# The last image's opening and end, a projection written by halves, and the outputs in other parts: one edit of a two-layer convolution kernel

## Chip, cores and metric

The kernel runs on one core of a Trainium2 chip. The metric is the device time of one launch in microseconds (us). A core has TensorE (PE, matmuls; PEld is its weight loads), VectorE (DVE), ScalarE (ACT), GpSimd (POOL) and SyncE (SP, which here only issues DMAs), each with its own instruction stream. They meet through semaphores and share the on-chip memory SBUF; matmul results arrive in PSUM, eight banks of 512 fp32 values on each of 128 partitions.

## What is computed

The input x has 4 images of 256 channels and 48 x 48 pixels. Two layers follow, each added to its input:

```python
# layer 0
h = relu(batch_norm(conv3x3(group_norm(x), conv_w) + conv_b))     # fixed statistics
q, k, v = qkv_w @ h + qkv_b                                       # 8 heads of 32 channels, N = 2304 pixels
a = softmax(q.T @ k * 32**-0.5) @ v
x = x + proj_w @ a + proj_b
# layer 1
g = group_norm(x)
w = conv3x3(g, W_cat)                                             # 45 logits a pixel
outs = [g] + [sum over 9 taps of shift(g, tap * d) * softmax(w[9 of d])[tap] for d in (1, 6, 12, 24, 36)]
y = W_scale @ concat(outs)                                        # 1x1 convolution over 6 * 256 channels
x = x + (y - mean(y)) * rsqrt(var(y) + eps) * gamma + beta        # mean and var over all 4 images
```

The statistics of y run over all images, so no output can be made before the last image's y is finished. Everything is fp32.

## The kernel before, in words

**Halves and chunks.** The 256 channels lie as two halves (index `o` or `h`, `NH` = 2) on 128 partitions. The pixels go in `NCK` = 6 chunks of 8 rows (`CH` = 384 pixels). A tile such as `pp` or `py` is `[P, 2, 512]` or `[P, 3, 512]` in PSUM: half 0 in its first bank, half 1 in its second.

**Order of work.** For each image in turn: attention (`attention`), then the dynamic filters of layer 1 (`dynamic_filters`). During the dynamic filters of images 0 to 2, TensorE also works off the convolution and qkv of the next image (the generator `other`, called through `run` and `fill`). The last image (`alone`) has no such work beside it. The order of all instructions is written out by hand (`manual_schedule`); inside the dynamic filters a small planner (`clock`) keeps a due time for each engine and chooses from them who does what. The semaphore waits are put in by the framework from the tiles that instructions read and write. A fallback for very large scores (`general`) is compiled into the same program, but not run here.

**Attention.** Queries go in 9 units of up to 512; the last unit holds the remaining 256 of both channel halves. In each of 18 key steps, `scores` makes the scores (L954), ScalarE exponentiates them (L962, L963), and `weigh` multiplies by the values (L983). The sum of the exponentials is kept by VectorE in `acc` (L999); in up to five of the steps, part of it is added by a DMA into a scratch tile instead, which L1006 adds later. `sums` (L1015) then sums `acc` over keys with a matmul by ones. In the last unit the last step's exponentials go to `sums` directly. `close` transposes, inverts and multiplies (L1024 to L1034).

**Projection.** `project` (L1067, L1076) makes layer 0's output for one chunk: for both halves two matmuls each, and then for each half the addition of bias and input, its group-norm statistics, and a store. Per image, five of the six chunks are done inside attention, at step 6 of units 3, 5, 7 (two chunks) and 8; the sixth needs the last unit and comes at the opening of `dynamic_filters`.

**Opening of the dynamic filters.** The sixth projection; loading ScalarE's Sqrt table; the group norm's finish (`Norm.finish`: aggregates, two small matmuls into a `misc` bank at L617 to L628, and the inverse root, L87 to L89); loading the Exp table; normalizing (L592); and the first chunk's logits and softmax (`weights`, L1137 onwards). In images 0 to 2, conv work stands in between.

**Taps.** For each chunk, each dilation and each tap: the weight is broadcast into PSUM (`wb`, L1406 or ScalarE's L1403), VectorE multiplies (L1463), GpSimd adds into `cat` (L1480). Three other ways: the first tap writes `cat` (L1437); a *single* product goes to the 1x1 convolution directly; a *split* tap has its second half multiplied and added by VectorE (L1445 to L1449) and its first half added by GpSimd (L1452). A tap is split if GpSimd's due time is past VectorE's by more than `SPLIT` = 4500 ns. `mix` (L1290) is the 1x1 convolution, accumulated in `py`. After the chunk's last one, `done` copies `py` away (L1315, L1317) and takes the statistics (L1323).

**End.** After the last chunk, `finish` aggregates the statistics (L157), makes scale and shift (L87 to L161), and then for images 0 to 3 scales on ScalarE (L1568), adds the residual on VectorE (L1579, L1586) and stores. Images 0 and 1 go in pieces of a channel half (2304 pixels), the first half in pieces of 384. Images 2 and 3 go by chunks. Shortly before, the residual of image 3 and four chunks of image 2's y are loaded (L1500, L1504).

Of the kernel before, what the change touches and what calls it, by code (L numbers as in the profile page):

```python
# [16 lines left out]
N = HH * WW  # L17
P = 128
# [30 lines left out]
def conv_preact_kernel(  # L49
# [98 lines left out]
        nc.vector.tensor_tensor(bn_t, bn_t, vec[:, BN_B, :], ALU.add)  # L148
        return bn_s, bn_t

    def batch_norm_of(yst, pool, tag):

        ymv = pool.tile([P, NH, 2], F32, tag="ymv", name=f"ymv_{tag}")
        ysc = pool.tile([P, NH], F32, tag="ysc", name=f"ysc_{tag}")
        ysh = pool.tile([P, NH], F32, tag="ysh", name=f"ysh_{tag}")
        for o in range(NH):
            nc.vector.bn_aggr(ymv[:, o, :], yst[:, o].rearrange("p c s -> p (c s)"))  # L157
# [374 lines left out]
    with tc.tile_pool(name="w", bufs=1) as wpool, tc.tile_pool(  # L532
# [36 lines left out]
        lg = wpool.tile([P, CH], F32, tag="lg", name="lg")  # L569
        nc.gpsimd.memset(lg, 0.0)  # L570
        yst = wpool.tile([P, NH, B * NCK, 6], F32, tag="yst", name="yst")
        bn_s6 = wpool.tile([P, NH], F32, tag="bn_s6", name="bn_s6")


# [349 lines left out]
        qkv = {}  # L924
        CONV_QKV = MM * (6 * 4 * 6 * TN / CH + NCK * NH * 4 + NT * 2 * C / CH)

        def attention(b, q, k_, vT, pools, spare, project, scratch):


# [39 lines left out]
            def weigh(u, m, p):  # L969
                if m == 0:  # L970
                    state[u] = dict(
                        num=ps_a.tile([P, 512], F32, tag="num", name=f"num_{b}_{u}"),
                        acc=work0.tile([P, 4, QC], F32, tag="acc", name=f"acc_{b}_{u}"),
                    )
                st = state[u]
                several = len(units[u]) > 1
                if several and m == 0:

                    for j, r in enumerate(heads):
                        nc.tensor.matmul(st["num"][r, :], zeros, p[:, j, :], start=True, stop=False)  # L980
                for i, (g, q0, n, at) in enumerate(units[u]):
                    for j, r in enumerate(heads):
                        nc.tensor.matmul(  # L983
                            st["num"][r, at : at + n],
                            vT[:, m, g * P + j * D : g * P + (j + 1) * D],
                            p[:, j, at : at + n],
                            start=(m == 0 and not several),
                            stop=(m == NT - 1 and i == len(units[u]) - 1),
                        )
                end = u == last  # L990
                if end and m == NT - 1:
                    sums(u, p, True, False)
                elif m == 0:
                    st["first"] = p
                else:
                    other = st["first"] if m == 1 else st["acc"]
                    lend = u > 0 and m in LENT[: len(LENT) - end]
                    js = slice(0, 1 if lend else 4)
                    nc.vector.tensor_tensor(st["acc"][:, js], other[:, js], p[:, js], ALU.add)  # L999
# [19 lines left out]
            def close(u):  # L1019

                sums(u, state[u]["acc"], u < last, True)
                st = state.pop(u)
                t = scratch
                nc.vector.transpose(t, st["den"])  # L1024
                rc = work0.tile([P, QC // D], F32, tag="rc", name=f"rc_{b}_{u}")
                nc.vector.reciprocal(rc, t.rearrange("p (k d) -> p k d", d=D)[:, :, 0])
                nc.vector.transpose(
                    t.rearrange("p (k d) -> p k d", d=D),
                    rc.unsqueeze(2).to_broadcast([P, QC // D, D]),
                )  # L1030
                for g, q0, n, at in units[u]:
                    dst = ao[:, g, q0 : q0 + n]
                    src = dst if u < last else st["num"][:, at : at + n]
                    nc.vector.tensor_tensor(dst, src, t[:, at : at + n], ALU.mult)  # L1034
# [27 lines left out]
        def project(b, c, ao, pp, norm):  # L1062

            t = pads[b % 2]
            for o in range(NH):
                for g in range(NH):
                    nc.tensor.matmul(  # L1067
                        pp[:, o, :CH],
                        wp[:, g, o * P : (o + 1) * P],
                        ao[:, g, c * CH : (c + 1) * CH],  # L1070
                        start=(g == 0),
                        stop=(g == NH - 1),
                    )
            for o in range(NH):
                x1 = inside(t, o, c * R, R)
                nc.vector.scalar_tensor_tensor(  # L1076
                    out=x1, in0=rows_of(pp[:, o, :CH]), scalar=pbias[:, o : o + 1], in1=x1,
                    op0=ALU.add, op1=ALU.add,
                )
# [25 lines left out]
        def dynamic_filters(b, ao, chunk, norm, other, pools, beside):  # L1105
# [114 lines left out]
            alone = b == B - 1  # L1220
            ready = {}


            next(beside, None)
            while chunk < NCK:
                project(b, chunk, ao, ps_y.tile([P, 2, 512], F32, tag="y", name=f"pp_{b}_{chunk}"), norm)
                chunk += 1
            table(AF.Sqrt)
            run(2400)
            for at, _ in enumerate(norm.finish(misc)):  # L1230
                if at:
# [2 lines left out]
            for _ in beside:  # L1234
                pass
            table(AF.Exp)

            for r0, r1 in ((0, 2 * R + 1), (2 * R + 1, HH)):
                for h in range(NH):
# [41 lines left out]
            def mix(c, n, o, rhs, last=False, at=None):  # L1281
                def go():
# [13 lines left out]
                        )  # L1296
                    part = 1.0 if at is None else (l1 - l0) * (x1 - x0) / CH
                    clock("PE", NH * MM * part, slot("y", 1) if n == 0 and o == 0 else 0.0)
                    if last and o == NH - 1:
                        done(c)  # L1300
                return go

            def done(c):
                cols = slice(c * CH, (c + 1) * CH)
                if alone:
                    yc = homes[c]
                elif c < NCK - 1:
                    yc = work1.tile([P, NH, CH], F32, tag="y", name=f"y_{b}_{c}", bufs=1)
                of = py.pop(c)[:, :, :CH]
                if c == NCK - 1 and not alone:  # L1310


                    rows = gn[:, :, 1 : 1 + R, 1 : 1 + WW]
                    for o in range(NH):
                        nc.scalar.copy(rows[:, o], rows_of(of[:, o]))  # L1315
                else:
                    nc.scalar.copy(yc, of)  # L1317
                free["y"].append(clock("ACT", 800, clock.t["PE"]))
                if c < NCK - 1:
                    of = yc  # L1320
                    clock("DVE", 1100, free["y"][-1])
                for o in range(NH):
                    nc.vector.bn_stats(yst[:, o, b * NCK + c, :], of[:, o, :])  # L1323
                if alone:
                    return
                if c < NCK - 1:
# [37 lines left out]
            for c in range(NCK):  # L1364
# [21 lines left out]
                for j, (n, at, (k, oy, ox, y0, y1, x0, x1)) in enumerate(taps):  # L1386
# [18 lines left out]
                    else:  # L1405
# [79 lines left out]
                    if j + 1 == len(taps) or taps[j + 1][0] != n:  # L1485
                        for o in range(NH):
# [4 lines left out]
                                    n == len(DILATIONS) - 1,  # L1491
                                ),
                            ))
            while queue:
                fill(when(queue[0]))
                if queue:
# [62 lines left out]

        def finish(work1):  # L1560

            ysc, ysh = batch_norm_of(yst, small, "f")

            def image(b, o):
                return out[b, o * P : (o + 1) * P].rearrange("c r w -> c (r w)")
# [6 lines left out]
            for b, ty, tx in ((0, y_0, x1_0), (1, y_1, x1_1)):  # L1572
                for o in range(NH):

                    n = CH if b == 0 and o == 0 else N
                    for c in range(0, N, n):
                        y = ty[:, o, c : c + n]
                        scaled(y, o)
                        nc.vector.tensor_tensor(y, y, tx[:, o, c : c + n], ALU.add)  # L1579
                        nc.sync.dma_start(out=image(b, o)[:, c : c + n], in_=y)  # L1580
            for b, ty, tx in ((2, y_2, x1_2), (3, homes, x1_3)):
                for c in range(NCK):
                    cols = slice(c * CH, (c + 1) * CH)
# [251 lines left out]
```

## Time and profile before

| | before |
|---|---|
| time, median of 3 runs | 2888.27 us (2886.0 to 2889.01) |
| profiled execution | span 2883.7 us, mean granted TensorE clock 0.981 |
| busy | PE 94%, DVE 83%, ACT 58%, POOL 41% |
| attention of the last image | about 2208 to 2586 us |
| last image's dynamic filters | about 2586 to 2847 us |
| outputs | about 2849 to 2880 us |

A group of instructions in the profile is named by its line, engine, operation and tiles (out<-in), with the number of instructions (x), busy time and mean duration. A timeline row gives start, duration of the merged group, and in brackets how long the engine had been idle and what ended that. fp32 matmuls appear as two records each. PEclk is the clock granted to TensorE, 1.00 being full speed. Idle time counts only where the engine is the one that others wait for.

### The profile page before, as it was taken

The numbers are of one execution on the slowest core, as the hardware profiler recorded it, in microseconds if no ns is written. First come the engines' busy times: TensorE is split into PE (matmuls) and PEld (weight loads), VectorE is DVE, ScalarE is ACT, GpSimd is POOL, SyncE is SP. The second block draws the span as 40 slices with busy tenths as digits, with TensorE's granted clock in tenths as the row PEclk, the third lists the DMA queues.
The fourth block names the chain that finished last, engine by engine and source line by source line (L and its number), as shares of the span: only waits on it lengthen the run. The fifth ranks groups of instructions, "written<-read, shape, count | busy, mean of one in ns | idle before, by whom it ended". The sixth has DMA issues, their size and how long they took to land. (4 is left out here: it accounts for less than half of the span.)

```text
span 2883.7 us, 43644 instructions
## 1 busy us (share of the span) xinstructions
PE 2721.6 (94%) x16950; PEld 1199.6 (42%) x16950; DVE 2381.2 (83%) x2570; ACT 1671.8 (58%) x2105; POOL 1187.6 (41%) x1000
## 2 busy tenths in 40 slices
PE   7999999899999999999999999999999999989994
PEld 5722224556542222455662222355654222244562
DVE  6488888789879988878977898978986988987886
ACT  3488888322349888712238888842234888861124
POOL 1000000798840010399890001079985001006893
PEclk9999999999999999999999999999999999999997
DMA  4524445132353444323225444423223345435225
GB/s 171 126 64 100 98 99 112 48 88 85 71 105 82 103 105 110 78 65 89 54 56 116 98 95 110 100 62 88 65 56 69 75 98 113 100 80 217 57 70 207
DMA packets 148199, 272.94 MB, mean 95 GB/s; under 512 B 66760, under 2 KB 117008, under 8 KB 146192
## 3 DMA queue, kind: packets, MB, share of 16 engines
q0 software_dynamic: 23264, 128.10, 19.5%
q1 hardware_dynamic: 82384, 87.31, 10.8%
q10 hardware_dynamic: 42336, 54.66, 7.5%
q8 instruction: 135, 2.21, 0.3%
q14 instruction: 80, 0.66, 0.1%
HBM read 115.02 MB, written 32.33 MB: 51 GB/s over the span
## 5 line engine op out<-in xcount | busy, mean ns | idle before, releaser
L999 DVE TENSOR_TENSOR acc<-acc,p 128x2048 f32<-128x2048 f32 (+1 forms) x572 | 1061.2, 1855 | 116.3 <-ACT p L963 66.5
L1480 POOL TENSOR_TENSOR cat<-cat,prod 128x752 f32<-128x752 f32 (+9 forms) x661 | 883.3, 1346 | 142.0 <-DVE prod L1463 105.5
L963 ACT ACTIVATE p<-se 128x1536 f32<-128x1536 f32 x648 | 938.5, 1448 | 0.0
L954 PE MATMUL so<-q,k 32*128 32x512 f32 (+1 forms) x1440 | 731.2, 595 | 23.5 <-ACT p L962 17.1
L954 PE MATMUL se<-q,k 32*128 32x512 f32 (+1 forms) x4320 | 740.0, 595 | 0.0
L983 PE MATMUL num<-p,vT 128*32 128x512 f32 (+1 forms) x5760 | 705.4, 562 | 4.3 <-ACT p L963 2.4
L1463 DVE TENSOR_TENSOR prod<-wb,pad 128x384 f32<-128x384 f32 (+8 forms) x687 | 482.7, 737 | 92.7 <-POOL cat L1480 51.3
L962 ACT ACTIVATE p<-so 128x512 f32<-128x512 f32 x648 | 388.4, 599 | 198.1 <-PE se L954 84.7
L954 PEld LDWEIGHTS so<-q,k 32*128 32x128 f32 x1440 | 217.1, 184 | 542.6 <-ACT p L962 494.4
L1003 POOL DMA_DIRECT2D scratch<-p x124 | 105.6, 852 | 766.7 <-ACT p L963 571.1
L1290 PE MATMUL py<-cat,wsc 128*128 128x384 f32 x960 | 348.9, 493 | 9.1 <-POOL cat L1480 7.8
L1403 ACT COPY wb<-ws 128x384 f32<-128x384 f32 (+3 forms) x260 | 121.7, 468 | 365.7 <-DVE prod L1463 243.8
L983 PEld LDWEIGHTS num<-p,vT 128*32 128x32 f32 x5760 | 133.1, 108 | 479.9 <-issue 446.9
L1406 PE MATMUL wb<-w,pick 128*128 128x384 f32 (+3 forms) x628 | 299.8, 511 | 18.9 <-DVE prod L1463 10.4
L1001 POOL DMA_DIRECT2D scratch<-p x32 | 17.9, 559 | 570.7 <-ACT p L963 360.4
L954 PEld LDWEIGHTS se<-q,k 32*128 32x128 f32 x4320 | 227.7, 184 | 4.4 <-ACT p L963 4.1
L1290 PEld LDWEIGHTS py<-cat,wsc 128*128 128x128 f32 x960 | 175.8, 191 | 113.9 <-POOL cat L1480 24.3
L1406 PEld LDWEIGHTS wb<-w,pick 128*128 128x128 f32 x628 | 116.9, 191 | 130.2 <-DVE prod L1463 51.4
L851 PE MATMUL pc<-cv_q,u 128*128 128x288 f32 x576 | 159.8, 411 | 7.1 <-DVE cv_q L742 6.4
L1137 PE MATMUL pg<-pad,wcat 128*45 128x384 f32 x864 | 160.7, 504 | 4.5 <-DVE pad L592 4.5
L851 PE MATMUL pc<-cv_k,u 128*128 128x288 f32 x576 | 156.8, 410 | 4.2 <-ACT m L797 2.4
L884 PE MATMUL pq<-hid,wqkv 128*128 128x384 f32 x384 | 136.6, 494 | 11.5 <-DVE yt L786 11.2
(224 smaller groups left out, 2311.8 us busy)
## 6 DMA issues: line engine op xcount, KB each, us to landing
scratch<-p POOLq DMA_DIRECT2D x156, 768.0 KB, 5.7
ws<-w_d ACTq DMA_DIRECT2D x256, 192.0 KB, 3.2
pad<-in_x SPq DMA_DIRECT2D x14, 1152.0 KB, 14.9
u<-u_d SPq DMA_DIRECT2D x18, 768.0 KB, 4.7
x_d<-pad SPq DMA_DIRECT2D x48, 192.0 KB, 2.6
xst<-in_x SPq DMA_DIRECT2D x36, 192.0 KB, 2.3
y_d<-y SPq DMA_DIRECT2D x15, 384.0 KB, 3.4
u_d<-u SPq DMA_DIRECT2D x6, 768.0 KB, 3.7
```

What stands on the lines that cost most here:

```text
L851: nc.tensor.matmul(m, u[:, h, kx, o * P : (o + 1) * P], halves[g][:, h, i, :, kx : kx + WW], start=(h == 0 and kx == 0), stop=(h == NH - 1 ...
L884: nc.tensor.matmul(pq[:, :CH], wqkv[:, i, s, g * P : (g + 1) * P], hid[:, i, cols], start=(i == 0), stop=(i == NH - 1),)
L954: nc.tensor.matmul(dst[:, at : at + n], k_[r, g, m * P : (m + 1) * P], q[r, g, q0 : q0 + n], start=True, stop=True,)
L962: nc.scalar.activation(p[:, 0, :], s1, AF.Exp, scale=QS)
L963: nc.scalar.activation(p[:, 1:, :], s3, AF.Exp, scale=QS)
L983: nc.tensor.matmul(st["num"][r, at : at + n], vT[:, m, g * P + j * D : g * P + (j + 1) * D], p[:, j, at : at + n], start=(m == 0 and not s ...
L999: nc.vector.tensor_tensor(st["acc"][:, js], other[:, js], p[:, js], ALU.add)
L1137: nc.tensor.matmul(pg[64 * s : 64 * s + NG, :CH], wcat[:, ii, k, :], window(gn, ii, cc * R, k // 3 - 1, k % 3 - 1), start=(i == 0 and k == 0),
L1290: nc.tensor.matmul(to, wsc[:, n * NH + i, o * P : (o + 1) * P], rhs(i), start=(n == 0 and i == 0), stop=(last and i == NH - 1),)
L1406: nc.tensor.matmul(pw[:, : nr * WW], pick[:, k : k + 1].to_broadcast([P, P]), w[:, l0 * WW : l1 * WW], start=True, stop=True,)
L1463: nc.vector.tensor_tensor(pv, wb, src, ALU.mult)
L1480: nc.gpsimd.tensor_tensor(dst, dst, pv, ALU.add)
```

## The change

The edit has seven parts. Most of them concern the last image, where no other work fills TensorE's pauses.

- `busy`: matmuls whose result is not used. Five after the last `sums` of the last image, four after its sixth projection (`warm(4)`), three after its Exp table load (`warm(3)`). They are to keep TensorE's clock up.
- In every image's last attention unit, the last two steps' exponentials instead of one go to `sums` directly, without VectorE's addition.
- `project` adds half 0 before half 1's matmuls are issued, in all 24 projections.
- `done` is called for each half. In the last chunk of the last image it takes a half's statistics from PSUM before the half is copied, and aggregates them at once; `finish` gets the aggregates (`ymv`).
- In the last dilation of the last chunk the split's threshold is 0 instead of 4500 ns.
- The Sqrt table for the last inverse root is loaded before the remaining `mix` work.
- Images 0 and 1 are stored in pieces of 768 pixels, the first two pieces being 384.

```diff
+        def busy(t, n):
+            for _ in range(n):
+                nc.tensor.matmul(t[:, :C], ident, wsc[:, 0, :], start=True, stop=True)
...
-                if end and m == NT - 1:
-                    sums(u, p, True, False)
+                if end and m > NT - 3:
+                    sums(u, p, m == NT - 2, False)
...
                 sums(u, state[u]["acc"], u < last, True)
+                if u == last and b == B - 1:
+                    busy(ps_a.tile([P, 512], F32, tag="one", name="warm"), 5)
...
                         stop=(g == NH - 1),
                     )
-            for o in range(NH):
                 x1 = inside(t, o, c * R, R)
...
             table(AF.Sqrt)
+            warm(4)
             run(2400)
...
             table(AF.Exp)
+            warm(3)
...
-                    if last and o == NH - 1:
-                        done(c)
+                    if last:
+                        done(c, o)
...
+                end = c == NCK - 1
+                if alone and end:
+                    nc.vector.bn_stats(yst[:, o, b * NCK + c, :], of[:, o, :])
+                    nc.vector.bn_aggr(ymv[:, o, :], yst[:, o].rearrange("p c s -> p (c s)"))
+                    nc.scalar.copy(homes[c][:, o], of[:, o])
+                if o < NH - 1:
+                    return
...
+                    ending = alone and c == NCK - 1 and n == len(DILATIONS) - 1
...
-                        and clock.t["POOL"] + added > clock.t["DVE"] + SPLIT
+                        and clock.t["POOL"] + added > clock.t["DVE"] + (0.0 if ending else SPLIT)
...
+            if alone:
+                table(AF.Sqrt)
             while queue:
...
-                    n = CH if b == 0 and o == 0 else N
-                    for c in range(0, N, n):
+                    c = 0
+                    while c < N:
+                        n = CH if b == 0 and o == 0 and c < 2 * CH else 2 * CH
```

More of the change, by code (lines that the diff above doesn't have):

```diff
@@ L149, in conv_norm, with batch_norm_of @@
         return bn_s, bn_t
-    def batch_norm_of(yst, pool, tag):
-        ymv = pool.tile([P, NH, 2], F32, tag="ymv", name=f"ymv_{tag}")
+    def batch_norm_of(yst, pool, tag, ymv=None):
         ysc = pool.tile([P, NH], F32, tag="ysc", name=f"ysc_{tag}")
         ysh = pool.tile([P, NH], F32, tag="ysh", name=f"ysh_{tag}")
-        for o in range(NH):
-            nc.vector.bn_aggr(ymv[:, o, :], yst[:, o].rearrange("p c s -> p (c s)"))
+        if ymv is None:
+            ymv = pool.tile([P, NH, 2], F32, tag="ymv", name=f"ymv_{tag}")
+            for o in range(NH):
+                nc.vector.bn_aggr(ymv[:, o, :], yst[:, o].rearrange("p c s -> p (c s)"))
         rstd_of(ysc, ymv[:, :, 1])
@@ L571, in conv_preact_kernel @@
         yst = wpool.tile([P, NH, B * NCK, 6], F32, tag="yst", name="yst")
+        ymv = wpool.tile([P, NH, 2], F32, tag="ymv", name="ymv")
         bn_s6 = wpool.tile([P, NH], F32, tag="bn_s6", name="bn_s6")
@@ L1073, in project @@
                     )
-            for o in range(NH):
                 x1 = inside(t, o, c * R, R)
@@ L1221, in dynamic_filters, with warm @@
             ready = {}
+            def warm(n):
+                if alone:
+                    busy(misc(f"warm_{b}_{n}"), n)
             next(beside, None)
@@ L1298, in go, with done @@
                     clock("PE", NH * MM * part, slot("y", 1) if n == 0 and o == 0 else 0.0)
-                    if last and o == NH - 1:
-                        done(c)
-                return go
-            def done(c):
+                    if last:
+                        done(c, o)
+                return go
+            def done(c, o):
+                of = py[c][:, :, :CH]
                 cols = slice(c * CH, (c + 1) * CH)
+                end = c == NCK - 1
+                if alone and end:
+                    nc.vector.bn_stats(yst[:, o, b * NCK + c, :], of[:, o, :])
+                    nc.vector.bn_aggr(ymv[:, o, :], yst[:, o].rearrange("p c s -> p (c s)"))
+                    nc.scalar.copy(homes[c][:, o], of[:, o])
+                if o < NH - 1:
+                    return
+                py.pop(c)
+                if alone and end:
+                    return
                 if alone:
                     yc = homes[c]
-                elif c < NCK - 1:
+                elif not end:
                     yc = work1.tile([P, NH, CH], F32, tag="y", name=f"y_{b}_{c}", bufs=1)
-                of = py.pop(c)[:, :, :CH]
-                if c == NCK - 1 and not alone:
+                if end:
                     rows = gn[:, :, 1 : 1 + R, 1 : 1 + WW]
@@ L1318, in done @@
                 free["y"].append(clock("ACT", 800, clock.t["PE"]))
-                if c < NCK - 1:
+                if not end:
                     of = yc
@@ L1325, in done @@
                     return
-                if c < NCK - 1:
+                if not end:
                     nc.sync.dma_start(out=y_d[b, :, :, cols], in_=yc)
@@ L1493, in dynamic_filters @@
                             ))
+            if alone:
+                table(AF.Sqrt)
             while queue:
@@ L1560, in finish @@
         def finish(work1):
-            ysc, ysh = batch_norm_of(yst, small, "f")
+            ysc, ysh = batch_norm_of(yst, small, "f", ymv)
             def image(b, o):
@@ L1580, in finish @@
                         nc.sync.dma_start(out=image(b, o)[:, c : c + n], in_=y)
+                        c += n
             for b, ty, tx in ((2, y_2, x1_2), (3, homes, x1_3)):
```

## The prediction

> **What bounds the kernel now.** I read four views: the page's busy row, the timeline of TensorE and VectorE around a projection, the same around the last image's opening, and the busy time in stretches for the attention and the tail.
>
> The page's first row and a stretch of the last image's attention (columns: busy PE, PEld, DVE, ACT, POOL, then granted clock, DMA share, GB/s):
>
> ```profile
> PE 2721.6 (94%) x16950; PEld 1199.6 (42%) x16950; DVE 2381.2 (83%) x2570; ACT 1671.8 (58%) x2105; POOL 1187.6 (41%) x1000
> ...
> 2400.00:2500.00 100.00, 99.44 (x748) 24.24 (x744) 89.47 (x61) 87.19 (x93) 9.33 (x12) 1.00 0.45 102
> ```
>
> TensorE is the bound, and in the attention it has 0.6 us of slack in 100. What it loses there is lost to the kernel.
>
> A projection inside the attention, timeline of TensorE, then VectorE:
>
> ```profile
> 2551.55 2.85 PE L1067 MATMUL pp<-ao,wp 128*128 128x384 f32 x8
> ...
> 2554.43 0.62 DVE L1076 SCALAR_TENSOR_TENSOR pad<-pp,pbias,pad 128x384 f32<-128x384 f32 x1 [2.63 <-PE pp L1067]
> ```
>
> Both halves take 2.85 us without a pause; VectorE, idle for 2.63 us, adds the first half only when both are done.
>
> How finely waits on a PSUM tile are drawn: the closing copies of image 0, ScalarE, then VectorE:
>
> ```profile
> 833.40 0.86 ACT L1315 COPY pad<-py 128x384 f32<-128x384 f32 x2 [8.57 <-PE py L1290]
> ...
> 834.29 1.03 DVE L1323 BATCH_NORM_STATS2 yst<-py 128x6 f32<-128x384 f32 x2 [7.60 <-ACT pad L1315]
> ```
>
> The first statistics read half 0 of `py`. The copy of half 0, 0.48 us long, ended near 833.88, but they started at 834.29, when the copy of half 1 was done. So a wait is drawn on the two-bank tile as a whole, even between its banks.
>
> The last image's opening on TensorE, then two stretches of it:
>
> ```profile
> 2582.81 1.07 PE L1015 MATMUL den<-acc,ones 128*32 128x512 f32 x8 [0.81 <-DVE acc L999]
> 2586.63 4.51 PE L1067 MATMUL pp<-ao,wp 128*128 128x384 f32 x8 [2.75 <-DVE ao L1034]
> 2594.01 0.59 PE L617 MATMUL pm_n<-mvn,gmat 128*128 128x2 f32 x2 [2.87 <-DVE mvn L614]
> ...
> 2597.45 7.87 PE L1137 MATMUL pg<-pad,wcat 128*45 128x384 f32 x36 [1.45 <-DVE pad L592]
> ...
> 2585.00:2590.00 5.00, 3.37 (x6) 1.98 (x7) 1.45 (x3) 0.00 (x0) 0.00 (x0) 0.70 0.00 0
> 2595.00:2600.00 5.00, 3.55 (x11) 1.78 (x13) 3.65 (x6) 2.04 (x5) 0.00 (x0) 0.50 1.06 404
> ```
>
> The 2.75 us gap costs the clock: the projection takes 4.51 instead of 2.85, the logits 7.87 where images 1 and 2 show 34 of the 36 records in 6.00.
>
> The tail, VectorE and two stretches:
>
> ```profile
> 2845.45 1.03 DVE L1323 BATCH_NORM_STATS2 yst<-py 128x6 f32<-128x384 f32 x2 [7.55 <-ACT wqkv L1317]
> 2846.40 1.45 DVE L157 BATCH_NORM_AGGREGATE ymv_f<-yst 128x2 f32<-128x144 f32 x2
> ...
> 2856.00:2858.00 2.00, 0.00 (x0) 0.00 (x0) 2.00 (x2) 2.00 (x2) 0.00 (x0) 0.50 0.01 4
> ...
> 2866.00:2874.00 8.00, 0.00 (x0) 0.00 (x0) 6.74 (x9) 7.76 (x13) 0.00 (x0) 0.50 1.00 360
> ```
>
> Once the outputs flow, the DMA engines are the limit (share 1.00, 360 GB/s), but they stand empty around 2857 while the first 2304-wide pieces are made.
>
> **What the Trainium skill says.** "TensorE: Matmul & The Clock Gate", Part 1: half rate after an idle window of about 3.4 us, full rate after a busy one. The trace agrees (0.50 from 2595 to 2600). "PSUM — Partial Sum Buffer", PSUM bank collisions: different banks may be used by two engines at once; so the wait between halves seen above is the program's, not the chip's. "ScalarE: Activation LUTs", What ACT_TABLE_LOAD costs: about 1283 ns; the trace has 1.28 us. "DMA: Bandwidth & Descriptors", Specifications: 435 GB/s for the fabric; the trace peaks there (433 GB/s at 2842 to 2844).
>
> **The change, part by part.**
>
> *Projection by halves* touches 24 projections, 20 of them inside attention. Half 1's matmuls now come after half 0's addition in program order. If the wait is on the whole tile, they wait for that addition to have read half 0. In time from the projection's first matmul: half 0 is done at about 1.49 (half 1 starts at 1.39 today); the addition (0.60) runs from 1.53 to 2.13, VectorE being free by then (it is done with earlier work between 0.25 and 1.54 in every projection that stands alone, L999's ends against L1067's starts); half 1 starts at 2.22 instead of 1.39. Loss 0.83 us each. Queued behind: the next scores, on which ScalarE's exponentials wait. TensorE has no slack there to pay it back: 20 x 0.83 = 16.6, less a little for its few existing waits, 15.5.
>
> *One step more summed by TensorE* (every image). The last accumulator addition but one, 2.29 us of VectorE, becomes four more matmuls, 1.07 us, of which 0.60 falls into a gap that stands there. The wait for `acc` before L1015 is 1.36, 0.45, 0.86 and 0.81 us in the four images; less 0.47 that gives 0.89, 0, 0.39 and 0.34.
>
> *Openings of images 0 to 2.* They gain those 1.3, and lose 0.8 each at their own projection, 2.4. The chain after it is ordered by TensorE's conv work (3.56 us), so earlier statistics bring nothing. The pause also falls into the window that would have warmed the clock; one window more at half rate costs at most 1.7 each (half of 3.4). The trace does not tell which; between 0 and 5.1 I take 2.4. Sum +3.5.
>
> *Last image's opening.* `den` ends at 2583.5; five fill matmuls of 256 columns run to 2585.7 (0.43 each: L1067's 384-column records, two to a matmul, are 0.324 us apart when warm, times 256/384, times 2); the projection starts at 2586.3, warm: half 0 to 2587.8, addition, half 1 from 2588.5 to 2590.0. VectorE: addition, statistics, two aggregates (0.60 + 0.56 + 0.48), 2591.7; the four fill matmuls end then too, so they delay nothing. Today that point is 2594.0, so 2.3 won. The norm's chain (2.66 to L592) shortens by about 0.5 with a warm TensorE (L617's two records take 0.28 us in image 2, 0.59 here). Logits from 2594.7, at 5.9: done at 2600.6 instead of 2605.3. Gain 4.7, less 0.2 for the three fill matmuls should they come late: 4.5. If the clock falls all the same, 2.5.
>
> *The tail.* With the lower threshold all five last taps of dilation 36 are split: the planner's due time of POOL is 2.8 us past VectorE's at the first. POOL then has 4 x 0.39 + 1.00 instead of 4 x 0.59 + 1.80, so it ends 1.6 us sooner; but TensorE is busy with the previous `cat` until 2840.8, so its last mix starts 0.9 sooner. Half 0 takes 1.4; its statistics 0.56 and its copy 0.48 now stand before half 1 (whole-tile wait again), then 1.4, 0.56 and one aggregate 0.75. L87 comes at 2846.2 instead of 2847.9: 1.7. The earlier Sqrt table load keeps 1.28 us out of that chain; today it is hidden beside the statistics. Outputs in pieces of 768 close the hole at 2854 to 2858: 9.44 MB at 376 GB/s (mean of 2858 to 2880) are 25.1 us, but x1 and y of earlier images are still being loaded to about 2850, so the last store lands near 2876 instead of 2880.2. ScalarE, at 25.0 us of scaling from 2847.4, plus an addition and a store, gives the same. Gain of the whole tail 4.2 (3.3 to 5).
>
> Sum: +15.5 + 3.5 - 4.5 - 4.2 = +10.3, so 2888.3 + 10.3 = 2898.6.
>
> **Rivals.** (1) *Halves are independent.* Then half 1 never waits: no attention loss, openings 0 to 2 gain 1.3, the last opening 5.4, the tail 5: 2876.6, faster. For it: the banks are separate, and the edit is meant so. Against: the 834.29 row, and that all 24 first additions waited for both halves. In the program of before, that statistic's wait count is also the one which only the second copy reaches. And the fallback branch, whose loop has the new order already, has half 1's matmul wait for half 0's addition. (2) *The waits are there but absorbed.* If TensorE's later waits in attention (23.5 us before L954, 17.1 of them on ScalarE) shrink in return, about half of the loss is left, 8, and openings 0 to 2 lose about 1: 8 + 1 - 8.7, so 2888.6, no change. Against: most of those waits hang on p buffers and DMAs which start after the projection, and move with it. (3) *The clock adds to it*: the three openings stay cold a window longer, 5.1 rather than 2.4, and the last is not warmed, 2.5 rather than 4.5: 2903.
>
> **How the numbers follow.** Forecast 0.60, (1) 0.10, (2) 0.17, (3) 0.13. The time is the forecast's, 2898.6. The bounds: TensorE's loss 14 to 17, openings 1 to 6, gains 6 to 10.5. From 2888 to 2906 leaves out (1), half of (2) and a little of (3). Within 0.2% is 5.8 us: faster 0.10 from (1), same 0.16 from (2), slower 0.74.
>
> **What would show it.** Right: in attention L1076's first addition starts about 1.5 us after L1067's first matmul, and L1067 itself then waits about 0.8 us on `DVE pad L1076`, 24 times; attention stages 3 to 4.5 us longer per image; L1137's first 36 records in about 6 us in the last opening; no empty DMA stretch after 2850. Wrong: if L1067 still takes 2.85 in one piece, rival 1 holds; if it is broken up but attention is no longer, rival 2.

## The result, and the profile after

| | before | after |
|---|---|---|
| median of 5 runs, side by side | 2886.0 us | 2898.2 us (2897.05 to 2900.53) |
| ratio | | 1.0041, 95% interval 1.0027 to 1.0056 |
| profiled span, TensorE clock | 2883.7 us, 0.981 | 2895.3 us, 0.986 |

The kernel became slower, by 12.2 us in the medians, although its mean clock rose. In the new file, the lines of before are L1077 (projection's matmuls), L1085 (its addition), L608 (its statistics), L620 to L631 (norm), L1146 (logits), L1305 (`mix`), L1325 to L1327 (the last chunk's statistics, aggregate and copy), L1430 (ScalarE's copy of a loaded weight). L933 are the unused fill matmuls.

The page's first row, then, from the busy time in stretches, the part of the attention that was shown for before (columns as there):

```profile
PE 2730.6 (94%) x17006; PEld 1201.8 (42%) x17006; DVE 2375.4 (82%) x2580; ACT 1672.5 (58%) x2111; POOL 1185.0 (41%) x1000
```

```profile
2400.00:2500.00 100.00, 96.98 (x724) 23.45 (x720) 85.29 (x56) 84.35 (x90) 9.63 (x12) 1.00 0.49 104
```

TensorE's share of the span is the same; the loss doesn't show there. It shows in the stretch: of 100 us, 96.98 are busy instead of 99.44, at full clock.

A projection in the attention, timeline of TensorE and then VectorE, and the row of the table of waits (engine, tile and line, who was waited for: total us, times, longest):

```profile
2570.47 1.56 PE L1077 MATMUL pp<-ao,wp 128*128 128x384 f32 x4
2572.74 1.56 PE L1077 MATMUL pp<-ao,wp 128*128 128x384 f32 x4 [0.71 <-DVE pad L1085]
...
2572.07 0.62 DVE L1085 SCALAR_TENSOR_TENSOR pad<-pp,pbias,pad 128x384 f32<-128x384 f32 x1
```

```profile
PE pp L1077 <- DVE pad L1085: 17.3, 24, 0.8
```

The addition now starts 1.60 us after the first matmul, as intended. But the second four matmul records stand 0.71 us still, until that addition ends. The wait occurs 24 times, once for every projection.

The last image's opening on TensorE; below it ScalarE's first copy of a weight that a DMA loaded:

```profile
2601.55 2.43 PE L933 MATMUL warm<-wsc,ident 128*128 128x256 f32 x10
2604.36 1.53 PE L1077 MATMUL pp<-ao,wp 128*128 128x384 f32 x4 [0.39 <-DVE ao L1044]
2606.66 1.56 PE L1077 MATMUL pp<-ao,wp 128*128 128x384 f32 x4 [0.77 <-DVE pad L1085]
...
2610.01 0.38 PE L620 MATMUL pm_n<-mvn,gmat 128*128 128x2 f32 x2
...
2611.84 1.56 PE L933 MATMUL warm<-wsc,ident 128*128 128x256 f32 x6 [0.25 <-DVE grstd_n L87]
2613.46 6.21 PE L1146 MATMUL pg<-pad,wcat 128*45 128x384 f32 x36
...
2642.32 0.24 ACT L1430 COPY wb<-ws 128x96 f32<-128x96 f32 x1 [16.72 <-DMA ws<-w_d]
```

The fill matmuls keep the clock: the projection is warm, the logits take 6.21 instead of 7.87 us. From the projection's first matmul to the logits' last the opening takes 15.31 us instead of 18.70. The last row is what the forecast overlooked; in the profile of before it stands so:

```profile
2624.92 0.24 ACT L1403 COPY wb<-ws 128x96 f32<-128x96 f32 x1 [13.67 <-DMA ws<-w_d]
```

Counted from the last projection's first matmul (2604.36 and 2586.63), this copy starts at 37.96 after and 38.29 before. Of the 3.39 us won, 0.33 arrive there; ScalarE waits 3 us longer for the DMA instead.

The tail: TensorE's last matmuls, VectorE's last statistics, and from the busy time in stretches the emptiest 2 us of the outputs (DMA share and GB/s at the end):

```profile
2853.72 4.03 PE L1305 MATMUL py<-cat,wsc 128*128 128x384 f32 x12
2858.92 1.56 PE L1305 MATMUL py<-cat,wsc 128*128 128x384 f32 x4 [1.17 <-ACT wqkv L1327]
...
2857.79 0.57 DVE L1325 BATCH_NORM_STATS2 yst<-py 128x6 f32<-128x384 f32 x1 [3.64 <-PE py L1305]
...
2860.59 0.56 DVE L1325 BATCH_NORM_STATS2 yst<-py 128x6 f32<-128x384 f32 x1 [1.39 <-PE py L1305]
```

```profile
2866.00:2868.00 2.00, 0.00 (x0) 0.00 (x0) 2.00 (x3) 2.00 (x3) 0.00 (x0) 0.50 0.67 245
```

Half 1's last matmuls wait 1.17 us for half 0's copy, the same kind of wait. The emptiest output stretch still moves 245 GB/s where before one moved 4.

Where the time went, from the first matmul on. "Attention" is from an image's first score matmul to its last projection; "filters" from the logits' 36th record on.

| stretch | after minus before, us | forecast |
|---|---|---|
| attention, four images | +16.2 | +15.5 - 1.6 = +13.9 |
| openings and filters of images 0 to 2 | -3.9 + 5.1 = +1.2 | +2.4 + 2.4 = +4.8 |
| last opening and filter, to the first L87 of the end | -3.4 - 0.2 = -3.6 | -4.2 - 1.7 = -5.9 |
| from there to the last store | -2.6 | -2.5 |
| sum | +11.2 | +10.3 |

The forecast's 4.5 for the last opening holds 0.3 that fall ahead of the projection; here they stand with attention.

### The profile page after: what moved, and what is told of

Its sections match the earlier page's. It is cut to its first block, busy times and chain, and to the rows that moved or that the text cites. A ratio compares the mean times of both kernels' runs of the same rounds, so it can differ in the third digit from the quotient of the medians.

```text
span 2895.3 us, 43766 instructions
## 1 busy us (share of the span) xinstructions
PE 2730.6 (94%) x17006; PEld 1201.8 (42%) x17006; DVE 2375.4 (82%) x2580; ACT 1672.5 (58%) x2111; POOL 1185.0 (41%) x1000
## 5 line engine op out<-in xcount | busy, mean ns | idle before, releaser
L1305 PE MATMUL py<-cat,wsc 128*128 128x384 f32 x960 | 349.0, 493 | 9.5 <-POOL cat L1508 7.9
L1430 ACT COPY wb<-ws 128x384 f32<-128x384 f32 (+3 forms) x260 | 121.7, 468 | 373.4 <-DVE prod L1491 240.9
L1433 PE MATMUL wb<-w,pick 128*128 128x384 f32 (+3 forms) x628 | 300.2, 510 | 24.2 <-DVE prod L1491 15.5
L1009 POOL DMA_DIRECT2D scratch<-p x32 | 17.9, 559 | 568.3 <-ACT p L971 384.8
L1305 PEld LDWEIGHTS py<-cat,wsc 128*128 128x128 f32 x960 | 175.5, 191 | 114.8 <-POOL cat L1508 24.8
L1146 PE MATMUL pg<-pad,wcat 128*45 128x384 f32 x864 | 158.1, 498 | 1.2 <-DVE pad L595 0.9
L887 PE MATMUL pq<-hid,wqkv 128*128 128x384 f32 x384 | 137.9, 498 | 11.5 <-DVE yt L789 11.2
```

What stands on the lines that cost most here:

```text
L887: nc.tensor.matmul(pq[:, :CH], wqkv[:, i, s, g * P : (g + 1) * P], hid[:, i, cols], start=(i == 0), stop=(i == NH - 1),)
L1146: nc.tensor.matmul(pg[64 * s : 64 * s + NG, :CH], wcat[:, ii, k, :], window(gn, ii, cc * R, k // 3 - 1, k % 3 - 1), start=(i == 0 and k == 0),
L1305: nc.tensor.matmul(to, wsc[:, n * NH + i, o * P : (o + 1) * P], rhs(i), start=(n == 0 and i == 0), stop=(last and i == NH - 1),)
L1433: nc.tensor.matmul(pw[:, : nr * WW], pick[:, k : k + 1].to_broadcast([P, P]), w[:, l0 * WW : l1 * WW], start=True, stop=True,)
```

## The experiments

All were measured beside the kernel before, whose median was between 2882.5 and 2884.0 in these runs, so ratios are compared rather than times: 0.1% is 2.9 us. A difference of two ratios is uncertain by about 0.0011 to 0.0014, 3 to 4 us (the two intervals taken as independent). Theory W: the framework draws a wait on the two-bank tile as a whole, and 20 pauses in attention outweigh all gains.

**e1_undo and e2_own: is it the order, or the shared tile?** The first ("the undo" from here on) restores the old order, the second keeps the new one and gives each half a tile (in attention half 0 takes the bank of the first scores; in the opening it takes a bank of the broadcasts).

```diff
 # e1_undo
+            for o in range(NH):
                 x1 = inside(t, o, c * R, R)
 # e2_own
-                        pp[:, o, :CH],
+                        pp[o][:, :CH],
...
-                        pp = three(f"pp_{b}_{chunk}")
+                        pp = [ps_a.tile([P, 512], F32, tag="one", ...), three(f"pp_{b}_{chunk}")[:, 0]]
```

> The changed kernel with the project loop of before: both halves' matmuls first, then both additions. Theory W (whole-tile wait): each of 20 projections in attention loses its 0.88 us pause and about 0.1 us of refilling, 20 x 0.98 = 19.6 us; the last opening stays within 1 us; total 2898.2 - 19.6 = 2878.6 (2876 to 2881), and the attention stages fall back to the 375 to 379 us of before, less about 1 us each for the den matmuls. Rival A (the wait is absorbed and attention is longer for another reason, such as the extra den matmuls): 2895 to 2899. Rival C (the pause fills TensorE's idle windows in a way that keeps the clock elsewhere): attention falls by 19 but the filter stages gain nothing or lose, total above 2883.

> The changed kernel with its order of halves kept, but each half of the projection in a PSUM tile of its own. Theory W: the wait comes from the shared tile alone, so half 1 starts at about +1.4 after half 0 with no wait on DVE pad, half 0's addition still starts at about +1.5, and the time is that of the undo or up to 2 us better (the additions end 0.6 us sooner in four openings): 2876 to 2881. Rival O (the order of the additions costs by itself, since VectorE's first addition now comes ahead of other work): stays at 2893 to 2899.

Measured: e1_undo 2875.47, ratio 0.9974 (0.9964 to 0.9983); e2_own 2875.5, ratio 0.9972 (0.9961 to 0.9983). Against 1.0041 both are 0.67 to 0.69%, 19 to 20 us. A projection of e2_own, TensorE, then VectorE:

```profile
2549.45 1.56 PE L1077 MATMUL pa<-ao,wp 128*128 128x384 f32 x4
2550.84 1.45 PE L1077 MATMUL pp<-ao,wp 128*128 128x384 f32 x4
...
2551.05 0.62 DVE L1085 SCALAR_TENSOR_TENSOR pad<-pa,pbias,pad 128x384 f32<-128x384 f32 x1
```

Half 1 follows at 1.39 without a pause, while VectorE reads half 0 from the other bank. So the order costs nothing that these runs can tell; the shared tile costs it all. Rivals A, C and O fall. The early addition wins nothing measurable in attention either: e2_own is no faster than e1_undo, and in the undo's table of waits for the last image's attention no engine waits for that addition.

**e3_only: the halved loop alone, in the kernel before.**

```diff
-            for o in range(NH):
                 x1 = inside(t, o, c * R, R)
```

> The kernel before with nothing but the halved project loop. Theory W: 20 x 0.98 = 19.6 us in attention and about 0.9 us in each of four openings, 2886.0 + 19.6 + 3.6 = 2909 (2904 to 2912; the upper end if the openings stay cold longer). Rival A (absorbed): 2886 to 2890.

Measured: 2906.87, ratio 1.008 (1.0066 to 1.0094), 23 us slower. A projection of it on TensorE:

```profile
2570.68 1.56 PE L1067 MATMUL pp<-ao,wp 128*128 128x384 f32 x4
2572.95 1.56 PE L1067 MATMUL pp<-ao,wp 128*128 128x384 f32 x4 [0.71 <-DVE pad L1075]
```

The pause is the same. The time is theory W's, but its parts are not. Attention grows by 12.6 us in this trace, not by 19.6, and TensorE's waits for ScalarE's exponentials in it shrink from 21.5 to 15.2: here a third of the pause seems to be paid back, as rival 2 had it. (In the changed kernel they are 16.6 against 17.9 in the undo.) The four openings grow by 1.4, 4.4, 2.9 and 1.3 us, and their time at half clock from 4.7, 3.4, 5.2 and 10.2 to 8.6, 9.2, 9.0 and 15.7: alone, the pause goes with more half clock, as the forecast had supposed for the whole change.

**e4_undo_noden: the undo, and VectorE adds the last step but one again.**

```diff
-                if end and m > NT - 3:
-                    sums(u, p, m == NT - 2, False)
+                if end and m == NT - 1:
+                    sums(u, p, True, False)
```

> As the undo, and in addition the last accumulator step but one goes back from TensorE to VectorE (den summed by TensorE for the last step alone). Theory D (the den edit shortens the wait before the projection by what scores-to-projection shows, 9.11/8.20/8.62/8.55 to 7.54 in all four images, sum 4.3 us, and its extra TensorE work is what keeps the openings of images 0 and 1 warm): 4 us slower than the undo, openings 0 and 1 with 3 to 5 us of half clock each again. Rival D2 (what the openings gain the filters give back, as the pair before/after shows: opening plus filter of images 0 to 2 are net -0.1, +0.5, +0.8): within 1.5 us of the undo.

Measured: 2879.32 (20 runs), ratio 0.9986 (0.9979 to 0.9992), 3.5 us slower than the undo by the ratios, which is nearer to D but, at plus or minus 3.3, does not exclude D2. The trace shows D's first half: from the last score to the projection it is 9.11, 8.19, 8.54 and 8.49 us again, against 7.53 in the undo, 4.2 in all. The end of the last attention, TensorE, first two rows of before, then three of the undo:

```profile
2580.08 0.85 PE L983 MATMUL num<-p,vT 128*32 128x256 f32 x11 [0.60 <-ACT p L963]
...
2582.81 1.07 PE L1015 MATMUL den<-acc,ones 128*32 128x512 f32 x8 [0.81 <-DVE acc L999]
```

```profile
2573.08 1.04 PE L1023 MATMUL den<-p,ones 128*32 128x512 f32 x8
...
2575.16 1.03 PE L1023 MATMUL den<-p,ones 128*32 128x512 f32 x7
2575.66 1.39 PE L1023 MATMUL den<-acc,ones 128*32 128x512 f32 x8
```

The undo's first row is the new work. It lies where before had a gap of 0.60 for ScalarE and then 0.81 for `acc`, and its last row follows without a wait. D's second half, that this work warms openings 0 and 1, is not shown by this pair: opening 1 had no half clock in the undo and 3.4 us in this run, but opening 0 had some in both, and e6_oldpieces, which has the undo's edits up to the last image, had 6.2 and 3.4 (the last section says on what that hangs).

**e5_nofill: the undo without the fills.** The 12 fill matmuls, whose results nothing reads, are left out.

```diff
-            for _ in range(n):
+            for _ in range(0):
```

> The undo without the fill matmuls of the last image's opening (12 matmuls of 256 columns left out, whose results nothing reads). Theory F (the fills carry the last opening's gain): the opening goes back from 15.4 to about 18.5 us with some 10 us of half clock, so the kernel is 3.2 us slower than the undo: 2878.7 (2877 to 2880). Rival F2 (the den matmuls, 1.07 us more, or the moved clock windows do it): the opening stays at 15 to 16 us and the time within 1 us of the undo's 2875.5.

Measured: 2878.04 (21 runs), ratio 0.9981 (0.9974 to 0.9987), 2.0 us slower than the undo by the ratios, between the two theories and, at plus or minus 3.3, not clear of either. The opening in this run:

```profile
2585.92 4.51 PE L1077 MATMUL pp<-ao,wp 128*128 128x384 f32 x8 [2.74 <-DVE ao L1044]
...
2596.75 7.96 PE L1147 MATMUL pg<-pad,wcat 128*45 128x384 f32 x36 [1.45 <-DVE pad L595]
```

It takes 18.79 us against 15.43 in the undo, so in this pair the fills do all of the opening's 3.4. They don't always keep the clock: of ten traces with fills, five still have one 3.4 us stretch at half clock in this opening and take 15.7 to 16.8. From the projection to the end of the first chunk (its copy of `py`) it is 85.1 against 83.3: half is gone by then. ScalarE's first copy from `ws` is at 39.07 here and 37.34 in the undo. At the second chunk's copy this run is ahead, 128.0 against 129.0, and at L87 too, 257.6 against 258.6. So what of the fills' gain reaches the kernel's time is not shown.

**e6_oldpieces, e10_oldstats, e8_oldtail: the tail in parts.** The undo with the old output pieces; with the old statistics and table load; with the whole old tail (the split's threshold too).

```diff
 # e6_oldpieces, and in e8_oldtail
-                        n = CH if b == 0 and o == 0 and c < 2 * CH else 2 * CH
+                        n = CH if b == 0 and o == 0 else N
 # e10_oldstats, and in e8_oldtail
-                if alone and end:
+                if False:
                     nc.vector.bn_stats(yst[:, o, b * NCK + c, :], of[:, o, :])
...
-            if alone:
-                table(AF.Sqrt)
 # e8_oldtail
-                        and clock.t["POOL"] + added > clock.t["DVE"] + (0.0 if ending else SPLIT)
+                        and clock.t["POOL"] + added > clock.t["DVE"] + SPLIT
```

> The undo with the output pieces of before (one chunk at a time for the first half image, then 2304 wide). Theory P (the empty DMA stretch near 2857 is all that the tail gained): 2.5 us slower than the undo, 2878.0, and the empty stretch after the first chunks is back. Rival P2 (the pieces matter little because the earlier statistics do it): under 1 us.

> The undo with the last chunk's statistics, aggregates and table load as before (after both halves), the shared additions and the output pieces kept. Theory W in the tail (statistics by half on a shared tile win nothing, the 1.17 us wait eats them): from the last POOL addition to the first scaling 6.2 us as before, time within 0.3 us of the undo; all of the 1.53 us by which the first scaling came sooner is the shared additions'. Rival S (the early statistics carry it, the shares nothing): 1.5 us slower than the undo.

> The undo with the whole tail of before: threshold of the shared additions, statistics and aggregates of the last chunk after both halves, table load in its old place, output pieces. Theory S (shared additions and statistics by half save the 1.7 us before the first scaling that were forecast, and the pieces 2.5): 4.2 us slower than the undo, 2879.7. Rival S2 (the shares and statistics won nothing, only the pieces count): 2.5 us slower, 2878.0, equal to the run with the old pieces alone.

Measured: e6_oldpieces 2881.2, ratio 0.9991 (0.9983 to 0.9999); e10_oldstats 2877.41, ratio 0.9986 (0.9976 to 0.9997); e8_oldtail 2882.55, ratio 0.9995 (0.9986 to 1.0003). By the ratios they are 4.9, 3.5 and 6.1 us slower than the undo, each plus or minus about 4: the old pieces and the whole old tail do cost time, but their sizes can't be read from it, and the traces decide. From L87 to the end: 33.17 us in the undo, 33.15 in e10_oldstats, 35.61 in e6_oldpieces, 35.64 in e8_oldtail: the pieces are worth 2.4 to 2.5. The hole they close, in e6_oldpieces' stretches:

```profile
2851.00:2853.00 2.00, 0.00 (x0) 0.00 (x0) 1.20 (x1) 2.00 (x2) 0.00 (x0) 0.50 0.35 129
2853.00:2855.00 2.00, 0.00 (x0) 0.00 (x0) 2.00 (x2) 2.00 (x2) 0.00 (x0) 0.50 0.00 0
```

From a GpSimd operation that all have, its 1.00 us half of a tap ahead of the last dilation's, to L87: before 13.51, e8_oldtail 13.52, e10_oldstats 12.27, the undo 11.98, after 11.77. So the shared additions are worth 1.2, the statistics by half (with the earlier table load) 0.3 to 0.5, where 0.2 is the scatter of kernels with the same tail. Theory S holds in the sum (1.5 + 2.5 = 4.0).

**e7_ownlast: the undo with the last chunk's halves in tiles of their own.**

```diff
-                        py[c] = ps_y.tile([P, 2, 512], ...)
+                        t = ps_y.tile([P, 2, 512], ...)
+                        py[c] = [t[:, 0, :CH], t[:, 1, :CH]]
+                        if alone and c == NCK - 1:
+                            py[c][1] = misc(f"pz_{b}_{c}")[:, :CH]
```

> The undo with the last chunk's two output halves in PSUM tiles of their own, so that half 1's last mixing matmuls need not wait for half 0's statistics and copy. Theory W in the tail: the 1.17 us wait goes, the last aggregate ends about 1.0 us sooner and so does the end: 1 us faster, 2874.5. Rival T (the tail is set by the DMA engines, which are busy with earlier loads): no change, 0 to 0.3 us.

Measured: 2875.66 (5 runs), ratio 0.9966 (0.9952 to 0.9979); too wide to tell 1 us. TensorE's end in its trace, then VectorE:

```profile
2836.43 1.45 PE L1310 MATMUL py<-cat,wsc 128*128 128x384 f32 x4
2837.72 1.45 PE L1310 MATMUL pz<-cat,wsc 128*128 128x384 f32 x4
...
2837.92 0.57 DVE L1330 BATCH_NORM_STATS2 yst<-py 128x6 f32<-128x384 f32 x1 [3.63 <-PE py L1310]
```

The 1.17 us wait is gone, and the distance to L87 falls from 11.98 to 10.26, with L87 to the end unchanged (33.23). The statistics by half are worth 2.0 us when the halves are apart, and 0.3 when they share a tile.

**e9_best: everything kept, and both overlaps in tiles of their own** (the edits of e2_own and e7_ownlast together).

> The changed kernel with all its parts kept, and every pair of halves that the change overlaps in PSUM tiles of their own: the projection's and the last chunk's. Theory W: both waits go; as fast as the own-tile run plus the 1.5 to 1.7 us that the last chunk's own tiles showed between the last POOL addition and the first scaling: ratio to the kernel before 0.9966 (0.9955 to 0.9978), 2874 us. Rival: the gains do not add, since TensorE's clock falls at other places: 0.9972 to 0.9985.

Measured: 2873.59 (14 runs), ratio 0.9971 (0.9962 to 0.9979), 6 to 11 us faster than before, while the change as made was 12 slower. It keeps e7_ownlast's distance to L87 (10.27), but its ratio can't be told from that of the undo.

**e11_late and e12_late_nofill: the loads back, later.** SyncE issues some 12 MB of loads of the earlier images as soon as the last projection's stores are out. Here ScalarE issues them at their place in program order; e12_late_nofill also leaves out the fills.

```diff
                         def back():
-                                    nc.sync.dma_start(out=ty, in_=y_d[bb])
-                                nc.sync.dma_start(out=tx, in_=x1_d[bb])
+                                    nc.scalar.dma_start(out=ty, in_=y_d[bb])
+                                nc.scalar.dma_start(out=tx, in_=x1_d[bb])
```

> The kernel with all parts and own tiles, and in addition the loads back of the earlier images' y and residuals (12 MB, which SyncE issues as soon as the last projection's stores are out) issued by ScalarE instead, at their place in program order after the first chunk of the last image. Theory L (these loads hold up the first broadcast weights: ScalarE's first copy from ws comes 37 to 39 us after the last projection's first matmul in every run so far, with or without the fill matmuls): the copy comes by 30 us or sooner, the first chunk ends 4 us sooner, and the kernel is 2 to 5 us faster than without: 2870, ratio 0.9957. Rival L2 (the contention only moves to the second chunk): the first chunk ends sooner, the second later, time within 1.5 us of 2873.6.

> The same with the late loads but without the 12 fill matmuls. Theory L: with the loads out of the way, what the fills win in the opening (3.4 us) is no longer taken back before the first chunk's end, so this kernel is 3.4 us slower than the one with late loads and fills, where the pair with early loads differed by 1.7 us from the projection to the first chunk's end and by 2.6 us in the median. Rival L3 (something else takes it back, such as the clock): the pair differs by no more than 2 us again.

Measured: 2901.81, ratio 1.0063 (1.005 to 1.0077), and 2902.79, ratio 1.0068 (1.0054 to 1.0082). Both L and L2 missed: the kernel is slower, as the first chunk ends 26 us later (109.5 instead of 83.3 after the projection). ScalarE's first copy from `ws` in the timeline, of e9_best and then of e11_late, and the latter's row of the table of waits for that chunk and the following ones:

```profile
2618.76 0.24 ACT L1435 COPY wb<-ws 128x96 f32<-128x96 f32 x1 [15.10 <-DMA ws<-w_d]
```

```profile
2613.48 0.24 ACT L1435 COPY wb<-ws 128x96 f32<-128x96 f32 x1 [8.34 <-DVE prod L1496]
```

```profile
ACT wb L1435 <- DMA ws<-w_d: 47.2, 14, 22.4
```

The copy came at 28.7 us after the projection instead of 37.1, and no longer waited for a DMA: in the other kernels the loads do hold it up. The store of the weights landed after 1.7 us and the first 48 KB load of them after 2.8, against 6.8 and 9.8 in the changed kernel. The later copies of the chunk paid, one with 22.4 us: ScalarE had issued the 12 MB just ahead of their loads, and its next issue took 7.5 us. Whether the fills would keep their 3.4 us without the loads stays open: this pair differs by 1.0 in the medians and 1.5 at the first chunk's end, but the loads lie in the first chunk here too.

## Why the prediction was right, and where its terms were off

**The wait on the whole tile** decided it, as forecast: the addition at 1.60, the pause in all 24 projections, hardly any payback. The size: half 1 starts at 2.27, not 2.22, and the projection ends at 3.83 instead of 2.85. That is 0.98 us, not 0.83: 0.88 of later start, and 0.10 that the second half no longer overlaps the end of the first. 20 x 0.98 = 19.6, and the undo gave 19 back. Attention says the same: 1524.8 us in the changed kernel, 1501.3 to 1506.2 (mean 1504.8) in six traces with the old order and the rest of the edit up to there (e1, e5 to e8, e10). The forecast's 15.5 was 4 too low, as it took too short a pause and then a share for waits that would shrink. Rivals 1 and 2 are refuted for this change by the 17.3 us of waits and by attention.

**One step more on TensorE** was undervalued: 1.57, 0.66, 1.09 and 1.02 us from the last score to the projection (9.11, 8.20, 8.62 and 8.55 to 7.54 in all), 4.3 instead of 1.6. The failed term is "0.60 falls into a gap": all 1.07 us fell into waits, so nothing had to be subtracted from the wait for `acc`.

**Openings of images 0 to 2.** The forecast had them colder; two were warm (half clock 4.7, 3.4 and 5.2 us before, 0, 0 and 3.4 after). Yet filter 0 gave it back: with one 3.4 us window at half clock it took 292.1 us before, with two 295.65 after. Neither is a lasting mark of the change; the last section shows what sorts them. The six traces named above have the same edits up to the last image, and in them opening 0 takes 19.1 to 23.4 us and filter 0 292.1 to 296.1. The sum of these three openings and filters is 931.6 to 934.8 us in them, 932.7 before and 933.8 after, so the +1.2 is within the scatter, and the forecast's +4.8 (937.4) would lie outside it.

**The last opening** gained 3.4 from the projection on, not 4.2. About 0.3 is missing ahead of the norm, where half 1 starts 2.30 after half 0, and 0.3 in the logits, 6.21 instead of 5.9. The rest are the last three fill matmuls. The norm's chain did get shorter with a warm TensorE, from 2.66 to 2.24 us between L620 and the start of the normalizing (L617 and L592 before). The normalizing on VectorE, before, then after:

```profile
2596.67 3.32 DVE L592 TENSOR_SCALAR pad<-pad,gmean_n,grstd_n 128x816 f32<-128x816 f32 x4
```

```profile
2612.25 3.32 DVE L595 TENSOR_SCALAR pad<-pad,gmean_n,grstd_n 128x816 f32<-128x816 f32 x4
```

Before, the logits follow the start of this row by 0.78 us, waiting for it. After, they follow by 1.21, without a wait: the three fills run from 2611.84 to 2613.40, and the logits start at 2613.46. The fills came late by 0.43, where the forecast allowed 0.2.

Of the opening's gain little reached the end of the chunk: from the projection to the first chunk's copy it is 84.45 before and 83.95 after. (The rest of the last image's 3.6 is 1.4 won in the second chunk, whose cause is open, and the tail's 1.7.) The step that failed is to carry the opening's gain through to the end without asking what its consumer waits for: the weights that come by DMA behind the loads.

**The tail**: -1.7 before L87 and -2.6 after it, against 1.7 and 2.5. The 1.17 us wait between halves was in the forecast.

The errors cancelled: attention cost 2.3 more than forecast, openings and filters of images 0 to 2 cost 3.6 less, the last image gained 2.3 less. The mechanism was forecast; that the time came within 0.4 us of 2898.6 is luck, since the kernel before also ran 2.3 us faster beside the change than in the runs that the forecast started from.

## What to carry to other kernels

Before splitting a loop to overlap one half's consumer with the other half's producer, look at what the waits are drawn on: if it is the tile, give each half its own, or the overlap turns into a pause. On a saturated engine price such a pause at its full length, times the number of passes (in e3_only's one trace a third seems to have come back). A gain ahead of a DMA-bound point is a gain only up to that point; see from which event the consumer counts. Don't ascribe a few microseconds at half clock in one trace to an edit before other launches show them too.

## What the runs showed of the hardware

VectorE reading one bank while TensorE writes another slowed neither: 0.62 us for the addition with and without overlap, 1.45 for half 1's matmuls in e2_own. This agrees with the Trainium skill, "PSUM — Partial Sum Buffer", PSUM bank collisions.

TensorE's half-clock stretches in these traces are 3.4 us or multiples of it when nothing else cuts them, which agrees with the window in "TensorE: Matmul & The Clock Gate", Part 1. In each trace all changes of the granted clock between its first and its last lie on one grid of 3.413 us, within 0.003. The grid falls differently against the work in each launch, and that sorts the scatter. In the eleven traces with the `den` edit, by the time from image 0's last projection to the next point of the grid:

| next grid point after | half clock in opening 0 | in filter 0 | filter 0 takes |
|---|---|---|---|
| 1.79 to 2.45 us (after, e2, e11, e5, e7) | 0 | 6.8 us | 295.7 to 296.1 us |
| 2.58 us (e12) | 0 | 3.4 us | 294.3 us |
| 2.78 to 3.23, and 0.28 us (e6, e1, e10, e8, e9) | 2.9 to 6.2 us | 3.4 us | 292.1 to 293.2 us |

Where the grid falls alike, the edits show: at 1.76 us e3_only, without the `den` edit, has 8.6 us of half clock in opening 0, and the changed kernel at 1.79 has none; in opening 2 e4_undo_noden at 2.18 has 5.6, and e8_oldtail at 2.10 and the undo at 2.38 have none. So the work on `den` does keep an opening warm there, though not at every position. For the last opening the grid lies at 0.33, 0.25 and 0.52 in the traces of before, the changed kernel and e5_nofill, and their half clock in it is 10.2, 0 and 10.2 us: there the fills do it. The five traces that keep a 3.4 us stretch in spite of the fills lie from 0.71 to 1.82.

Runs of one kernel lie 3 to 14 us apart, and the slower ones mostly have the lower mean clock (correlation -0.84 over the 31 runs of before beside the undo, -0.88 over the 21 of e5_nofill). Of an edit worth 1 or 2 us the trace's local distances tell more than the median.
